# Last stage of two bottleneck blocks: the second block's last convolution with seven products for eight, on pairs of tiles

## The chip, the cores and the metric

The kernel runs on one core of one Trainium2 chip. The metric is device time in microseconds (us) of one execution. Of the kernel before, three runs are given: 2117.68, 2118.75 and 2119.07 us, so the median is 2118.75. One execution was recorded by the hardware profiler. Its span, from the first to the last instruction, is 2116.9 us, and the time of that execution is 2118.65 us.

## What is computed

Two equal blocks follow one another. The input is 64 images of 1024 channels and 14 x 14 pixels, in fp32. A block is, with the names of the reference:

```python
out = relu(bn(conv(x, w1, b1, 1, 0), g1, be1))     # 1x1, 1024 -> 256 channels
out = relu(bn(conv(out, w2, b2, 1, 1), g2, be2))   # 3x3, 256 -> 256
out = bn(conv(out, w3, b3, 1, 0), g3, be3)         # 1x1, 256 -> 1024
out = softplus(residual_scale)[0] * out
return relu(x + out)
```

`bn` normalises each channel with the mean and the variance of the whole batch. So nothing after a convolution can be finished before that convolution's statistics are complete, and the kernel falls into stages.

## The kernel before

**Tiles.** Channels lie on the 128 partitions. A tile is two images, 392 pixels (`PX`), and there are 32 tiles (`T`). A tile of x has 8 slots of 392 pixels (`CS`), one for each 128 of the 1024 channels; it is 1568 KB. A tile of the 256-channel data has two slots (`MS`) and stays in SBUF for all images, in `y_all`.

**Stages.** First comes the first convolution of block 0. Then, for each block: the 3x3 convolution; the Gram stage (`gram`, `conv3_stats`), which gets the mean and variance of the last convolution's result from products of its input, without computing it; and the last convolution with the residual. In block 0 the last convolution of a tile and the first convolution of block 1 run interleaved (`fused`). In block 1 nothing follows, so the last stage is plain: `residual` for one tile after the other. That is the stretch from about 1774 us to the end.

**The plain last stage.** For each tile, `residual` loads the tile of x from DRAM (`load_x`, on SP's DMA queue, in a ring of five buffers, `bufs=5` in `xpool`), makes for each of the 8 output slots two matmuls over the two input slots (`conv3`), adds the scaled result to x on VectorE (L837), applies the relu with the shift on ScalarE (L838), and stores the whole tile in one DMA from GpSimd's queue (L841). `Psum(scope, ["ps"], ps=5)` gives this stage five PSUM banks. The first two slots of tile 0 (`made`) are computed ahead of the statistics' end.

**Seven products for eight.** Taking two output slots, two input slots and two groups of columns, the last convolution is a 2 x 2 by 2 x 2 block product. Winograd's form of Strassen's scheme gets it with 7 block products in place of 8, at the price of sums of weights (`combine_w3`, made once), sums of columns (t1 to t4, for each group of columns) and partial results that are copied out and added later. The class `Seven` has the order of the products, `stream` interleaves one item with the item before it:

```python
            yield from now.p1()
            if before is not None:
                yield from before.p3()
                yield from before.p4()
            yield from now.p6()
            if before is not None:
                before.end()
            yield from now.p2()
            yield from now.p5()
            yield from now.p7()
```

One PSUM bank, `y`, takes p1, p6, p7 and p4 one on top of the other, and between them ScalarE copies its partial sums away (`saved`, L365 with the instruction at L265). The bank `p` takes p5 and p3; bank `x` takes p2. In `Conv3`, which `fused` uses, an item is one q of four (output slots q and q + 4) of one tile, and its columns are the two halves of the tile, 196 pixels each. After p2, p5, p3 and p4 VectorE adds a bank to x (`add`, L373). GpSimd adds the copies to x: after p3 for the first row (L399), after p7 for the second (L394). `end` does both relus on ScalarE.

**What sets the order.** Matmuls, and ScalarE's instructions issued by `act`, keep the order of the program (`keep_in_program_order`). The other engines' instructions are put in order by a scheduler when the kernel is built, and each engine then works through its list strictly in that order. DMAs of one queue are issued in order too: one that waits holds up those behind it. Five tiles of x can be in SBUF at once; a load into a buffer waits for the store of the tile that had it.

Of the kernel before, what the change touches and what calls it, by code (L numbers as in the profile page):

```python
# [34 lines left out]
FP = mybir.dt.float32  # L35
# [47 lines left out]
def bottlenecks(ctx: ExitStack, tc: tile.TileContext, x, w1s, w2s, w3s, pars, out):  # L83
# [19 lines left out]
    class Psum:  # L103


        def __init__(self, scope, cycle, **bufs):
            self.pool = scope.enter_context(tc.tile_pool(name="psum", bufs=1, space=bass.MemoryType.PSUM))
            self.cycle, self.bufs = itertools.cycle(cycle), bufs
# [5 lines left out]
    def load_x(pool, b, t, parts=1):  # L114
        xt = pool.tile([P, CS, PX], FP, tag="x", name=f"x_{b}_{t}")
        n = CS // parts
        for i in range(parts):
            nc.sync.dma_start(
                out=xt[:, i * n : (i + 1) * n, :].rearrange("p s f -> p (s f)"),
                in_=(x[t] if b == 0 else mids[t])[:, i * n * PX : (i + 1) * n * PX],  # L120
            )
        return xt
# [18 lines left out]
    def combine_w1(pool, w):  # L141
        return combine(pool, "w1", [[w[:, o, h] for h in range(2)] for o in range(MS)])

    def combine_w3(pool, w):
        n = CS // 2
        return combine(pool, "w3", [[w[:, s, o * n : (o + 1) * n] for s in range(MS)] for o in range(2)])
# [120 lines left out]
    class Conv1(Seven):  # L267
# [72 lines left out]
        def after7(self):  # L340
            self.result(1, 1, self.p, self.saved("au3"))

    class Conv3(Seven):

        prefix = "c"

        def __init__(self, psum, pool, xt, q, ys, sums, w3, aff, to):
            self.psum, self.pool, self.xt, self.n = psum, pool, xt, PX // 2  # L350
            self.o, self.to = (q, q + CS // 2), to
            (a, s), (self.scale, self.shift) = w3, aff
            self.a, self.s = [[w[:, q] for w in row] for row in a], [w[:, q] for w in s]
            self.b, (self.t1, self.t2, self.t3, self.t4) = ys, sums
            self.u12 = pool.tile([P, PX], FP, tag="cu12", name="cu12", bufs=2)

        def product(self, bank, w, b, start):
            matmul(
# [9 lines left out]
        def part(self, row, i):  # L368
            return self.xt[:, self.o[row], i * self.n : (i + 1) * self.n]
# [34 lines left out]
        def end(self):  # L404
            for row in range(2):
                self.relu(row)
            if self.to is not None:
                nc.scalar.dma_start(out=self.to, in_=self.xt.rearrange("p s f -> p (s f)"))

    def plain_conv1(psum, t, xt, a, par, stats):  # L410

# [413 lines left out]
        nc.vector.tensor_mul(sq, r[:, :, 1], r[:, :, 1])  # L825
        nc.vector.tensor_sub(mv[:, :, 1], r[:, :, 2], sq)

    def residual(psum, pool, b, t, w3, aff, made=()):

        scale, shift = aff  # L830
        xt = load_x(pool, b, t)
        to = mids[t] if b == 0 else out[t]
        step = 2 if b == 1 and t == T - 1 else CS
        for o in range(CS):
            ps = made[o] if o < len(made) else conv3(psum, t, o, w3)
            v = xt[:, o, :]
            nc.vector.scalar_tensor_tensor(v, ps, scale[:, o : o + 1], v, ALU.mult, ALU.add)  # L837
            nc.scalar.activation(v, v, AF.Relu, bias=shift[:, o : o + 1])  # L838
            if (o + 1) % step == 0:
                queue = nc.gpsimd if step == CS else nc.sync  # L840
                queue.dma_start(  # L841
                    out=to[:, (o + 1 - step) * PX : (o + 1) * PX],
                    in_=xt[:, o + 1 - step : o + 1, :].rearrange("p s f -> p (s f)"),
                )
        return xt

    def fused(psum, pool, xpool, first, w1, w3, aff, par, stats):


        xs = [first, load_x(xpool, 0, 1)]  # L850

        def last_convs():
            for t in range(1, T):
                if t + 1 < T:
                    xs.append(load_x(xpool, 0, t + 1))
                ys = [[two(t, s)[:, i * H // 2 : (i + 1) * H // 2] for i in range(2)] for s in range(MS)]
                sums = []
                for i in range(4):
                    v = pool.tile([P, PX // 2], FP, tag=f"ct{i}", name=f"ct{i}", bufs=2 if i > 1 else 1)
                    sums.append(v.rearrange("p (h l) -> p h l", l=G * W))  # L860
                t1, t2, t3, t4 = sums
                nc.vector.tensor_sub(t3, ys[1][1], ys[0][1])
                nc.vector.tensor_add(t2, t3, ys[0][0])
                nc.vector.tensor_sub(t1, ys[0][1], ys[0][0])
                nc.vector.tensor_sub(t4, ys[1][0], t2)
                for q in range(CS // 2):
                    yield Conv3(psum, pool, xs[t], q, ys, sums, w3, aff, mids[t] if q == CS // 2 - 1 else None)

        def first_convs():
            for t in range(T):  # L870
                yield Conv1(psum, pool, xs[t : t + 1], (t,), w1, par, stats)

        a, c = stream(first_convs()), stream(last_convs())
        for i in range(LAG):
            next(c)
        while True:
            more = next(a, "end"), next(c, "end")
            if more == ("end", "end"):
                break

    def stats_tile(n, name):
        return keep.tile([P, n, T, nc.vector.BN_STATS_DIM], FP, tag=f"stats{n}", name=name)
# [115 lines left out]
    for b in range(2):  # L998
        pb = par[b]
        sp = softplus(pb)  # L1000
        ccol = keep.tile([P, MS], FP, tag="ccol", name="ccol")
        nc.vector.tensor_scalar(ccol, pb[:, BE2 : BE2 + MS], 0.0, None, ALU.max)
        aff = affine(aggregate(stats1, T - 3 + b), MS, pb, G1, BE1)
        stats2 = keep.tile([P, MS, 1 + PARTS, nc.vector.BN_STATS_DIM], FP, tag="stats2", name=f"stats2_{b}")
        with tc.tile_pool(name=f"conv2_{b}", bufs=1) as pool, ExitStack() as scope:
            conv2(Psum(scope, ["ps"], ps=8), pool, b, pb, aff, stats2)

        with tc.tile_pool(name=f"last_{b}", bufs=1) as one, tc.tile_pool(
            name=f"last_x_{b}", bufs=4 if b == 0 else 5
        ) as xpool:  # L1010
            w3 = load_w3(one, b)
            if b == 0:
                w1 = load_w1(one, b + 1)
            aff = affine(aggregate(stats2, 0), MS, pb, G2, BE2)
            with ExitStack() as scope:
                if b == 0:
                    psum = Psum(scope, ["cy", "ay", "cx", "cy", "ay"], cy=2, ay=2)
                else:
                    psum = Psum(scope, ["ps"], ps=5)
                with tc.tile_pool(name=f"gram_{b}", bufs=1) as pool:  # L1020
                    crow = pool.tile([P, M], FP, tag="crow", name="crow")
                    nc.sync.dma_start(out=crow, in_=pars[b][:, NPAR:])
                    tc.keep_in_program_order(nc.vector.tensor_scalar(crow, crow, 0.0, None, ALU.max))

                    def piece(s, o):
                        spare = [xpool.tile([P, CS * PX], FP, tag="x", name="spare") for i in range(2)]
                        filters(1, s, o, spare)

                    weights = []
                    beside = {}  # L1030
                    if b == 0:
                        beside = {2 + 12 * i: partial(piece, i // MS, i % MS) for i in range(MS * MS)}
                        beside[NT - 5] = lambda: weights.extend((combine_w1(one, w1), combine_w3(one, w3)))
                    grams = gram(psum, pool, aff, crow, beside)
                    made = [conv3(psum, 0, o, w3) for o in range(2)]
                    mv3 = small.tile([P, CS, nc.vector.BN_AGGR_DIM], FP, tag="mv3", name="mv3")
                    conv3_stats(psum, pool, xpool, grams, w3, ccol, mv3)
                aff = affine(mv3, CS, pb, G3, BE3, conv_bias=B3)
                for a in aff:
                    nc.vector.tensor_scalar(a, a, sp, None, ALU.mult)  # L1040
                first = residual(psum, xpool, b, 0, w3, aff, made)
                if b == 1:
                    for t in range(1, T):
                        residual(psum, xpool, b, t, w3, aff)
                    return
                stats1 = stats_tile(MS, f"stats1_{b + 1}")
                with tc.tile_pool(name=f"conv1_{b + 1}", bufs=1) as pool:
                    fused(psum, pool, xpool, first, *weights, aff, par[b + 1], stats1)


# [39 lines left out]
```

## Time and profile before

| | |
|---|---|
| Median of three runs | 2118.75 us (2117.68 to 2119.07) |
| The profiled execution | 2118.65 us, its span 2116.9 us |
| TensorE, matmuls | 2068.3 us busy, 98% of the span |
| TensorE, weight loads (beside the matmuls) | 1747.9 us, 83% |
| VectorE | 1433.2 us, 68% |
| ScalarE | 814.2 us, 38% |
| GpSimd | 243.5 us, 12% |
| Mean DMA rate | 189 GB/s |
| L837, scaled add of a bank to x, 392 elements | 256 times, 626 ns |
| L838, relu, 392 elements | 264 times, 622 ns |
| Stores of the last stage (L841), 1568 KB each | 31, median 7.1 us to landing |
| Loads of x in the last stage, 1568 KB each | 32, median 7.6 us to landing |

How to read the profile: PE is TensorE's matmuls and PEld its weight loads, DVE is VectorE, ACT ScalarE, POOL GpSimd, SP the engine that only issues DMAs. A row of a group of instructions gives the line of the kernel, the engine, the operation, what it writes and reads with its shape, how often it ran, its busy time and the mean duration of one, and behind the last bar the time that the engine had been idle before such instructions, with what ended that wait. A row in order of time starts with the start in us and the duration in us; in brackets is the idle time ahead of it. An fp32 matmul is made of two passes and appears as two records.

### The profile page before, as it was taken

How to read it: one execution, taken by the hardware profiler on the slowest of the kernel's cores; microseconds unless marked ns; L12 is line 12 of the kernel's file. 1: busy time of each engine (PE TensorE's matmuls, PEld its weight loads, DVE VectorE, ACT ScalarE, POOL GpSimd, SP SyncE). 2: the span in 40 equal slices, each digit the busy share in tenths (PEclk: the TensorE clock that was granted, in tenths of full speed). 3: DMA queues.
4: the chain of work that ended last, by engine and by line, in shares of the span. 5: the costliest groups of instructions: out<-in, count | busy, mean ns of one | idle time of the engine just before them, and what ended most of it. 6: DMA issues, size and time to landing. Idle time of an engine off the chain costs nothing.

```text
span 2116.9 us, 27185 instructions
## 1 busy us (share of the span) xinstructions
PE 2068.3 (98%) x10368; PEld 1747.9 (83%) x10368; DVE 1433.2 (68%) x2778; ACT 814.2 (38%) x1579; POOL 243.5 (12%) x342
## 2 busy tenths in 40 slices
PE   8999989999989999999999999899999899999999
PEld 4555549999989889999999999799999897555555
DVE  5766559988866666666766667798888544444444
ACT  2211115233226055555555555523223402444444
POOL 0100000000001023333333333000000000000000
PEclk9999999999999999999999999999999999999999
DMA  7665425555543434444444443355554402778785
GB/s 292 250 211 209 163 90 192 201 191 184 200 159 118 155 150 159 177 183 161 175 160 176 183 160 145 120 214 184 190 208 180 194 1 99 306 277 325 282 321 215
DMA packets 45011, 400.00 MB, mean 189 GB/s; under 512 B 5584, under 2 KB 5840, under 8 KB 12240
## 3 DMA queue, kind: packets, MB, share of 16 engines
q1 hardware_dynamic: 30528, 280.28, 37.0%
q0 software_dynamic: 8448, 66.07, 7.7%
q10 hardware_dynamic: 5904, 51.91, 5.9%
q8 instruction: 82, 1.34, 0.3%
q14 instruction: 49, 0.40, 0.1%
HBM read 280.79 MB, written 117.44 MB: 188 GB/s over the span
## 4 chain that ended last, share of the span: by engine, by line
PE 93%; DVE 3%; ACT 2%; DMA 1%; issue 1%; POOL 0%; SPq 0%; DVEq 0%; ACTq 0%
PE ps L155 17%; PE ps L573 17%; PE ay L155 14%; PE ps L550 8%; PE cy L155 8%; PE ap L155 8%; PE ax L155 4%; PE cp L155 4%; PE ps L560 3%; PE cp L755 3%; PE cx L155 2%; PE ap L756 2%; ACT y L427 1%; PE ps L773 1%; DMA y<-in_w 0%
## 5 line engine op out<-in xcount | busy, mean ns | idle before, releaser
L573 PE MATMUL ps<-r,u 128*128 128x224 f32 (+1 forms) x2048 | 391.2, 343 | 14.1 <-DVE r L506 14.1
L573 PEld LDWEIGHTS ps<-r,u 128*128 128x128 f32 x2048 | 372.1, 190 | 18.9 <-DVE r L506 7.9
L155 PE MATMUL ps<-y,w 128*128 128x392 f32 x1024 | 340.5, 496 | 0.0
L155 PEld LDWEIGHTS ps<-y,w 128*128 128x128 f32 x1024 | 195.9, 191 | 143.5 <-issue 2.8
L837 DVE SCALAR_TENSOR_TENSOR x<-ps,scale,x 128x392 f32<-128x392 f32 x256 | 160.0, 626 | 175.5 <-PE ps L155 171.8
L265 ACT ACTIVATE cu<-cy,scale 128x196 f32<-128x196 f32 x372 | 154.0, 423 | 221.2 <-PE cy L155 221.2
L838 ACT ACTIVATE x<-x,shift 128x392 f32<-128x392 f32 x264 | 163.6, 622 | 183.7 <-DVE x L837 183.7
L155 PE MATMUL ay<-at,w1s 128*128 128x196 f32 (+1 forms) x752 | 209.7, 382 | 1.2 <-ACT au L265 1.0
L605 ACT ACTIVATE ms<-ps 128x448 f32<-128x448 f32 (+1 forms) x80 | 40.5, 506 | 333.7 <-PE ps L550 323.3
L155 PEld LDWEIGHTS ay<-at,w1s 128*128 128x128 f32 x752 | 136.0, 190 | 36.6 <-ACT au L265 4.6
L550 PE MATMUL ps<-sums,u 128*128 128x224 f32 (+1 forms) x768 | 158.6, 337 | 0.0
L265 ACT ACTIVATE x<-x,shift 128x392 f32<-128x392 f32 x248 | 140.9, 614 | 28.3 <-POOL x L399 28.3
L399 POOL TENSOR_TENSOR x<-x,cu 128x392 f32<-128x392 f32 x124 | 125.9, 1015 | 188.1 <-DVE x L373 188.0
L373 DVE SCALAR_TENSOR_TENSOR x<-cp,scale,x 128x196 f32<-128x196 f32 x248 | 103.4, 417 | 63.7 <-PE cp L155 63.7
L550 PEld LDWEIGHTS ps<-sums,u 128*128 128x128 f32 x768 | 131.5, 189 | 0.1
L155 PE MATMUL cy<-ct,w3s 128*128 128x196 f32 x496 | 123.0, 330 | 1.4 <-ACT cu L265 1.4
L755 PE MATMUL cp<-zt 128*128 128x257 f32 x392 | 120.6, 389 | 2.9 <-DVE zt L775 2.4
L265 ACT ACTIVATE au<-ay 128x196 f32<-128x196 f32 (+1 forms) x141 | 53.8, 381 | 167.2 <-PE ay L155 164.6
L155 PE MATMUL ap<-x,w1s 128*128 128x196 f32 (+1 forms) x376 | 107.7, 390 | 5.4 <-DVE y L311 5.4
L427 ACT ACTIVATE y<-y,shift,scale 128x1568 f32<-128x1568 f32 (+2 forms) x68 | 103.6, 1584 | 5.6 <-DVE shift L934 5.6
L155 PE MATMUL ax<-x,w 128*128 128x196 f32 (+1 forms) x376 | 104.8, 381 | 0.0
L155 PE MATMUL ay<-x,w 128*128 128x196 f32 (+1 forms) x376 | 104.8, 381 | 0.0
(226 smaller groups left out, 3429.2 us busy)
## 6 DMA issues: line engine op xcount, KB each, us to landing
x<-in_x SPq DMA_DIRECT2D x62, 1568.0 KB, 6.6
u<-u SPq DMA_DIRECT2D x64, 1280.0 KB, 5.5
x<-mid SPq DMA_DIRECT2D x32, 1568.0 KB, 7.6
mid<-x ACTq DMA_DIRECT2D x31, 1568.0 KB, 5.1
out<-x POOLq DMA_DIRECT2D x31, 1568.0 KB, 7.1
u<-u SPq DMA_DIRECT2D x32, 1024.0 KB, 4.8
u<-y POOLq DMA_DIRECT2D x16, 320.0 KB, 6.2
u<-spare POOLq DMA_DIRECT2D x16, 320.0 KB, 2.7
```

What stands on the lines that cost most here:

```text
L155: tc.keep_in_program_order(nc.tensor.matmul(*args, **kw))
L265: tc.keep_in_program_order(nc.scalar.activation(*args, **kw))
L373: nc.vector.scalar_tensor_tensor(v, bank, self.scale[:, o : o + 1], v, ALU.mult, ALU.add)
L399: nc.gpsimd.tensor_add(v, v, self.u12)
L427: nc.scalar.activation(y, y, AF.Relu, bias=shift[:, s : s + 1], scale=scale[:, s : s + 1])
L550: nc.tensor.matmul(to[:, o, :n], u[:, s, o, k], v[:, s].rearrange("p l c -> p (l c)"), start=(s == 0), stop=(s == MS - 1),)
L560: nc.tensor.matmul(to, u[:, s, o, k], v, start=(s == 0), stop=(s == MS - 1))
L573: nc.tensor.matmul(to, u[:, s, o, k], v, start=start, stop=stop, skip_group_check=by_slot)
L755: nc.tensor.matmul(g0, zt[:, c, 0:P], zt[:, c, :], start=first, stop=last)
L756: nc.tensor.matmul(g1, zt[:, c, P:M], zt[:, c, P:], start=first, stop=last)
L837: nc.vector.scalar_tensor_tensor(v, ps, scale[:, o : o + 1], v, ALU.mult, ALU.add)
L838: nc.scalar.activation(v, v, AF.Relu, bias=shift[:, o : o + 1])
```

## The change

The last stage is rewritten for tiles 1 to 30. Tiles 0 and 31 stay plain.

- `final` takes the tiles in 15 pairs. A pair's columns are its two tiles, 392 pixels each, so `Conv3Pair` is `Conv3` with n = 392 in place of 196. There are four items for a pair, one for each q, and an item has seven products.
- The column sums t1 to t4 become a function, `column_sums`, that both stages use. In the last stage they are 392 elements wide, and made once for a pair.
- `Conv3Pair.after3` has GpSimd add the two copies to x in two instructions of 392, since the two tiles are not one piece of memory. `after7` is inherited: another add of 392 on GpSimd.
- `Conv3Pair.end` does the relu of the first row on ScalarE, two instructions of 392, and that of the second row on VectorE, two `tensor_scalar` (add the shift, maximum with 0).
- The stores go out per item: for each of the two tiles one DMA of the two slots q and q + 4 (392 KB, rows of 1568 bytes), on SP's queue. Before it was one DMA of 1568 KB per tile on GpSimd's queue.
- Five loads of x are issued ahead; after the first item of each pair, loads up to four tiles ahead of the pair's first are issued.
- PSUM in this stage has banks cy (2), cx (2), cp (2), and single ones for the Gram stage; the plain tiles draw on cy and cx, four banks, where they had five.
- `combine_w3` is now also made for block 1, beside the Gram stage, at its fifth step from the end.

```diff
+    def column_sums(pool, ys, n):
+        sums = []
+        for i in range(4):
+            v = pool.tile([P, n], FP, tag=f"ct{i}", name=f"ct{i}", bufs=2 if i > 1 else 1)
+            sums.append(v.rearrange("p (h l) -> p h l", l=G * W))
+        t1, t2, t3, t4 = sums
+        nc.vector.tensor_sub(t3, ys[1][1], ys[0][1])
+        nc.vector.tensor_add(t2, t3, ys[0][0])
+        nc.vector.tensor_sub(t1, ys[0][1], ys[0][0])
+        nc.vector.tensor_sub(t4, ys[1][0], t2)
+        return sums
...
+    class Conv3Pair(Conv3):
+        def part(self, row, i):
+            return self.xt[i][:, self.o[row], :]
+
+        def after3(self):
+            self.add(0, 1, self.p)
+            for i in range(2):
+                v = self.part(0, i)
+                nc.gpsimd.tensor_add(v, v, self.u12[:, i * self.n : (i + 1) * self.n])
+
+        def end(self):
+            for i in range(2):
+                o, v = self.o[0], self.part(0, i)
+                act(v, v, AF.Relu, bias=self.shift[:, o : o + 1])
+            for i in range(2):
+                o, v = self.o[1], self.part(1, i)
+                nc.vector.tensor_scalar(v, v, self.shift[:, o : o + 1], 0.0, ALU.add, ALU.max)
+            q, step = self.o[0], CS // 2
+            for i in range(2):
+                nc.sync.dma_start(
+                    out=self.to[i].rearrange("p (s f) -> p s f", s=CS)[:, q::step, :], in_=self.xt[i][:, q::step, :]
+                )
...
+    def final(psum, pool, xpool, xs, a, w3, aff):
+        def pairs():
+            for t in range(1, T - 1, 2):
+                ys = [[two(t + i, s) for i in range(2)] for s in range(MS)]
+                sums = column_sums(pool, ys, PX)
+                for q in range(CS // 2):
+                    yield Conv3Pair(psum, pool, xs[t : t + 2], q, PX, ys, sums, w3, aff, out[t : t + 2])
+                    if q == 0:
+                        for i in range(len(xs), min(t + 5, T)):
+                            xs.append(load_x(xpool, 1, i))
+
+        for _ in stream(pairs()):
+            pass
+        residual(psum, xs[T - 1], 1, T - 1, a, aff)
...
-                    psum = Psum(scope, ["ps"], ps=5)
+                    psum = Psum(scope, ["cy", "cx"], cy=2, cx=2, cp=2)
...
+                    beside = {NT - 5: combined}
...
-                first = residual(psum, xpool, b, 0, w3, aff, made)
-                if b == 1:
-                    for t in range(1, T):
-                        residual(psum, xpool, b, t, w3, aff)
-                    return
+                xs = [load_x(xpool, b, t) for t in range(2 if b == 0 else 5)]
+                residual(psum, xs[0], b, 0, w3, aff, made)
+                with tc.tile_pool(name=f"rest_{b}", bufs=1) as pool:
+                    if b == 1:
+                        final(psum, pool, xpool, xs, w3, *weights, aff)
+                        return
```

## The prediction

> **What bounds the kernel now.** I read the page's busy shares first, then the table by stretches for the last stage (everything from about 1774 us on), then the order of time inside one tile of it, then the rows of single operations, and at last the places of the fused stage in the middle where GpSimd and VectorE work at once. Columns of the table: stretch, length, then busy us of TensorE, its weight loads, VectorE, ScalarE, GpSimd; granted clock, DMA share, GB/s.
>
> ```profile
> 1850.00:1900.00 50.00, 50.00 (x154) 28.85 (x153) 23.80 (x39) 23.62 (x38) 2.65 (x5) 1.00 0.78 294
> 1900.00:1950.00 50.00, 50.00 (x154) 28.85 (x152) 23.75 (x39) 23.62 (x38) 2.66 (x5) 1.00 0.85 316
> 1950.00:2000.00 50.00, 50.00 (x153) 28.88 (x152) 23.75 (x39) 23.62 (x38) 2.66 (x5) 1.00 0.77 280
> ```
>
> TensorE never rests, the others are half idle, and DMA is busy 0.77 to 0.85. Inside a tile:
>
> ```profile
> 1881.67 0.53 POOL L841 DMA_DIRECT2D out<-x  x1 [10.00 <-ACT x L838]
> 1882.72 0.63 DVE L837 SCALAR_TENSOR_TENSOR x<-ps,scale,x 128x392 f32<-128x392 f32 x1 [0.64 <-PE ps L155]
> 1884.04 0.63 DVE L837 SCALAR_TENSOR_TENSOR x<-ps,scale,x 128x392 f32<-128x392 f32 x1 [0.69 <-PE ps L155]
> 1892.20 0.53 POOL L841 DMA_DIRECT2D out<-x  x1 [10.00 <-ACT x L838]
> ```
>
> One store to the next is 10.53 us for a tile of 16 products: 0.658 us each. So the stage is bound by TensorE: a pair of tiles takes 21.06 us, and the 30 tiles that change take 315.9 us. The operations that the change uses:
>
> ```profile
> L265 ACT ACTIVATE x<-x,shift 128x392 f32<-128x392 f32 x248 | 140.9, 614 | 28.3 <-POOL x L399 28.3
> L399 POOL TENSOR_TENSOR x<-x,cu 128x392 f32<-128x392 f32 x124 | 125.9, 1015 | 188.1 <-DVE x L373 188.0
> L431 DVE TENSOR_SCALAR y<-y,scale,shift 128x896 f32<-128x896 f32 x2 | 1.5, 747 | 0.1
> L432 DVE TENSOR_SCALAR y<-y 128x896 f32<-128x896 f32 x2 | 1.3, 626 | 0.1
> ```
>
> And three places of the fused stage, in order of time:
>
> ```profile
> 753.12 0.96 DVE L338 TENSOR_TENSOR at<-x,at 128x784 f32<-128x784 f32 x1
> 753.43 1.11 POOL L394 TENSOR_TENSOR x<-x,cu 128x196 f32<-128x196 f32 x1 [2.07 <-ACT cu L265]
> 754.51 1.00 POOL L399 TENSOR_TENSOR x<-x,cu 128x392 f32<-128x392 f32 x1
> ...
> 1102.99 1.02 POOL L399 TENSOR_TENSOR x<-x,cu 128x392 f32<-128x392 f32 x1 [0.45 <-DVE x L373]
> 1103.82 0.41 DVE L863 TENSOR_TENSOR ct<-ct,y 128x196 f32<-128x196 f32 x1 [0.24 <-PE cy L155]
> 1104.26 0.36 DVE L865 TENSOR_TENSOR ct<-y,ct 128x196 f32<-128x196 f32 x1
> ```
>
> L394 takes 0.60 in the mean of its row, but 1.11 where a VectorE sum with both inputs in SBUF had begun 0.31 us before it: it stood until that sum was through. The reverse is L863: 0.41 where GpSimd was still at work, 0.35 to 0.36 for its like (L865) alone, in all 30 of its later rounds. So GpSimd lets VectorE in about 0.83 + 0.05 = 0.88 us after its own start. The scaled adds with one input in PSUM (L373) last 0.42 beside GpSimd or not.
>
> **What the Trainium skill says.** "SBUF — State Buffer", section "Who interferes with whom": GpSimd's only SBUF ports are VectorE's second pair; a VectorE instruction with two SBUF inputs, or one in a 2-port mode, and a GpSimd instruction exclude each other, the later one waits for the whole of the earlier. The rows above agree for two inputs (1.11 for 0.60). "VectorE: DVE Perf Modes", section "Mode 2×_2P": fp32 operations with one tensor and a scalar, SBUF to SBUF, run two results a cycle through that pair. L432 agrees: 626 ns for 896 elements is less than one a cycle. That such an operation also shuts GpSimd out, no place of this trace shows. "DMA: Bandwidth & Descriptors", section "Specifications": rows from 512 B up go at line rate. The packets of the trace agree roughly: median 469 ns for 12544 B, 124 for 3136, 84 for 2048, 46 for 1024.
>
> **The change part by part.** An item is a pair of tiles and one q of four: seven products p1 to p7.
>
> TensorE: 28 products for 32 per pair, 28 x 0.658 = 18.42 us for 21.06, which is 15 x 2.64 = 39.5 us less if it never waits.
>
> ScalarE per item: three copies out of PSUM (about 0.62, the duration of the same size in L838) and two relus, 5 x 0.62 = 3.1 of 4.61 us. It fits.
>
> VectorE per item: four scaled adds of 0.63 (0.535 when one follows the other: three of L837 took 1.69), two relus, and per pair four sums. A relu with one scalar from SBUF: L432 fits 896/1.92 + 160 ns, L431 has two such scalars and 120 more, so 204 + 160 + 60 = 0.42, 0.33 in a row. Sums of 392 lie between 0.50 (336) and 0.62 (448): 0.56, 0.475 in a row. Busy 4 x 0.535 + 0.66 + 0.475 = 3.3 of 4.61.
>
> GpSimd per item: three adds of 392 (V0, G11, V1), 3.05 us, 0.98 apart at best (754.51 less 753.43 + 1.11 is -0.03). Per pair that is 12.2 us, where the stage had nothing but issues.
>
> No engine is full, but they are chained, and orders are fixed. As built, VectorE has per item: A00 (add after p2), A11 (after p5), R11 (relu), A01 (after p3), A10 (after p4), R10 (relu); GpSimd has V0 (needs A00), G11 (needs A11 and ScalarE's copy after p7), V1 (needs A01). R11 needs G11. R10 comes up while V1 holds the ports. Next item's A00 stands behind R10. The round, with handovers of 0.09 VectorE to GpSimd (1102.91 to 1102.99) and 0.05 back: A00 0.63 + 0.09, V0 0.98, G11 1.02 + 0.05, R11 0.33, A01 0.63 + 0.09, V1's hold 0.88, R10 0.33: 5.03 us, over TensorE's 4.61. In a pair the sums come in twice: one between A10 and R10 of the third q, again after V1's hold (+0.48); three between A11 and A01 of the last, which take turns with V0 and G11 (counted from A00's end: the first waits for V0 until 0.97, G11 for it until 1.44, the second for G11 until 2.3, so A01 starts at 3.25 in place of 2.14 + 0.33 = 2.47: +0.75). Pair: 4 x 5.03 + 1.23 = 21.35 us, of 18.42 that TensorE needs. 15 x (21.35 - 21.06) = +4.4 us. What then is late is p3 of each item, which waits for A11, so TensorE idles some 0.7 us per item.
>
> Around it: the first two pairs' five sums are scheduled into the short chain of eight-element operations after the statistics (1774.24 to 1776.87), 5 x 0.5 = +2.5 us on the first add; with four banks for the plain tile where five stood, TensorE is through its two free banks at 1774.06 + 2.63 = 1776.7 and waits for the first add's end, 1777.5 + 2.5 = 1780.0: +3.4 us, none before. combine_w3 is four sums of 0.69 (2.5 in a row) in the Gram stage, where VectorE has 1.06 us idle of 1.75 and the copy's user another 0.86: +0.7.
>
> Stores and loads: 8 stores per pair on SP's queue between the loads, 128 packets of 1568 B per engine in place of 16 of 12544. Their time lies between 59 ns (in proportion to 12544) and 70 (to 1024); I take 66 between 46 and 84. Per pair and engine: loads 16 x 0.469 = 7.5, stores 128 x 0.066 = 8.4 (7.5 to 9.0), 15.9 of 21.35 us: hidden. A load waits on SP for the last stores of the tile whose buffer it takes, behind at most one store of the next pair; it is issued about an item into a pair and its tile is needed one to two pairs' starts later, some 14 us for the 7 that a landing takes. The last tile is as before: 0.
>
> Sum: +4.4 + 3.4 + 0.7 = +8.5, less about 1 us because the first items run at TensorE's pace before the round takes hold: +7.5. On the profiled span 2116.9 that is 2124.4; its own time was 1.75 above its span (2118.65), and the median of the runs 0.1 above that: 2126 us.
>
> **The rivals.** (1) The ports don't bind, or hardly. Then A01, A10, R10 follow at once (0.535 + 0.535 + 0.33 = 1.40, where A01, V1's hold and R10 made 1.93), the round is 4.5, TensorE's 4.61 rules with some 0.1 lost at its edges: 18.8 a pair, 15 x 2.26 - 4.1 = 30 us faster, 2089. Against it stands the 1.11 of L394. (2) The ports bind for relus alone, or are given back sooner than the 0.88: 19.6 to 20.1 a pair, 14 us faster, 2105. For it: the only long wait is a single one, and spans on GpSimd are rough. It decides below 20.8 us a pair, a round of about 4.9, only 0.13 from mine. (3) DMA becomes the bound: packets over (21.35 - 7.5) / 128 = 108 ns, or loads held up behind stores in one queue. At 130 ns a pair is 24.1: +46 + 4, 2168; a milder wait gives 2140 to 2150. For it: the share of 0.85 now, and one queue for both directions. Against: 124 ns is what twice the bytes took. (4) GpSimd's adds lengthen to 1.1 (beside the relus): the round 5.2, 2133. I count it with the main case.
>
> **How the numbers follow.** The forecast case 0.60 (own range 2115 to 2137), rival 1 0.07, rival 2 0.19, rival 3 0.14. I count 0.2% (4.2 us) as what a measurement can tell from none. Of the main case 0.06 falls below 2114.5, 0.16 within, 0.38 above 2123. So faster 0.06 + 0.07 + 0.19 = 0.32, same 0.16, slower 0.38 + 0.14 = 0.52. The range 2100 to 2144 leaves out rival 1, and tails of rivals 2 and 3.
>
> **What would show it.** Right: in the last stage TensorE busy about 0.86, pairs 21.3 us apart; p3 waiting for VectorE's L386; VectorE relus (L441) or sums that last far beyond 0.42 and 0.56 or begin late after GpSimd; GpSimd near 0.6 busy. Wrong: TensorE full with 18.5 us a pair (rival 1), L441 never above 0.45 beside GpSimd (rival 2), VectorE's adds waiting for x from DMA (rival 3).

## The result, and the profile after

The changed kernel takes 2124.0 us (median of four runs, 2122.6 to 2125.6) where the kernel before takes 2118.9 (2117.7 to 2121.2): 1.0023 times as long, 95% interval 1.0005 to 1.0040. That is slower, by little, and 2 us from the 2126 forecast. The profiled execution took 2125.6 us with a span of 2123.8.

The table by stretches for the last stage of the changed kernel, with the columns of the table shown for the kernel before:

```profile
1850.00:1900.00 50.00, 45.88 (x130) 23.33 (x128) 40.00 (x69) 26.43 (x48) 28.46 (x28) 1.00 0.82 293
1900.00:1950.00 50.00, 46.58 (x133) 24.36 (x134) 36.76 (x65) 25.99 (x47) 29.68 (x29) 1.00 0.81 287
1950.00:2000.00 50.00, 46.84 (x135) 24.27 (x133) 38.38 (x67) 27.42 (x49) 28.89 (x28) 1.00 0.87 313
```

TensorE, full before, has 130 to 135 matmul records in 50 us where it had 154; VectorE went from 23.8 to about 38 us, GpSimd from 2.7 to 29. No engine is full any more, and DMA's share (0.77 to 0.85 before) is much the same. What each engine waits for in the stage (window 1800 to 2100; engine, what waits, for whom: us in all, times, longest):

```profile
POOL x L433 <- DVE x L386: 119.6, 109, 1.5
ACT cu L265 <- PE cy L155: 108.6, 58, 2.2
DVE x L441 <- POOL x L407: 70.2, 43, 1.9
PEld cp L155 <- DVE x L386: 56.8, 56, 1.4
```

The waits make a ring: VectorE's relu R11 (L441) waits for GpSimd's G11 (L407), GpSimd's V0 and V1 (L433) for VectorE's adds (L386), and TensorE's p3 (its bank cp) for A11. One round of it in order of time, TensorE's and ScalarE's rows left out but for p3:

```profile
1941.67 0.61 DVE L386 SCALAR_TENSOR_TENSOR x<-cx,scale,x 128x392 f32<-128x392 f32 x1
1942.21 0.61 DVE L386 SCALAR_TENSOR_TENSOR x<-cp,scale,x 128x392 f32<-128x392 f32 x1
1942.42 1.01 POOL L433 TENSOR_TENSOR x<-x,cu 128x392 f32<-128x392 f32 x1 [0.89 <-DVE x L386]
1942.88 0.93 PE L155 MATMUL cp<-y,w3s 128*128 128x392 f32 x2 [0.70 <-DVE x L386]
1943.39 1.01 POOL L407 TENSOR_TENSOR x<-x,cu 128x392 f32<-128x392 f32 x1
1944.43 0.42 DVE L441 TENSOR_SCALAR x<-x,shift 128x392 f32<-128x392 f32 x1 [1.61 <-POOL x L407]
1944.78 0.62 DVE L386 SCALAR_TENSOR_TENSOR x<-cp,scale,x 128x392 f32<-128x392 f32 x1
1945.31 0.61 DVE L386 SCALAR_TENSOR_TENSOR x<-cy,scale,x 128x392 f32<-128x392 f32 x1
1945.47 1.02 POOL L433 TENSOR_TENSOR x<-x,cu 128x392 f32<-128x392 f32 x1 [1.07 <-DVE x L386]
1945.96 0.75 DVE L441 TENSOR_SCALAR x<-x,shift 128x392 f32<-128x392 f32 x1
1946.63 0.61 DVE L386 SCALAR_TENSOR_TENSOR x<-cx,scale,x 128x392 f32<-128x392 f32 x1
```

From A00 (cx) at 1941.67 to the next A00 at 1946.63 is 4.96 us, over the 4.61 that TensorE needs for seven products. The two relus are the thing to see: R11, with GpSimd at rest, takes 0.42; R10, come up while V1 is under way, takes 0.75. The groups of operations by shape say the same for the whole window (count | busy, mean ns | idle before):

```profile
L441 DVE TENSOR_SCALAR x<-x,shift 128x392 f32<-128x392 f32 x113 | 58.2, 515 | 71.6 <-POOL x L407 70.2
L353 DVE TENSOR_TENSOR ct<-y,ct 128x392 f32<-128x392 f32 x14 | 19.2, 1373 | 0.0
L352 DVE TENSOR_TENSOR ct<-y 128x392 f32<-128x392 f32 x14 | 15.7, 1124 | 0.0
L351 DVE TENSOR_TENSOR ct<-ct,y 128x392 f32<-128x392 f32 x14 | 15.0, 1068 | 0.0
L350 DVE TENSOR_TENSOR ct<-y 128x392 f32<-128x392 f32 x13 | 7.2, 553 | 0.0
```

A column sum that finds GpSimd at rest takes 0.55 (L350); the other three take up to 1.37, since they stand until a GpSimd add is through.

Below, "items" are the mean distances from one p3 to the next, for the first to the fourth q of a pair, read from the starts of p3 in the trace. In the changed kernel they are 4.96, 4.98, 5.48 and 5.83: a pair of 21.25 us, where two tiles took 21.06.

### The profile page after: what moved, and what is told of

Read it like the earlier page. It is cut to its first block, busy times and chain, and to the rows that moved or that the text cites. A ratio compares the mean times of both kernels' runs of the same rounds, so it can differ in the third digit from the quotient of the medians.

```text
span 2123.8 us, 27779 instructions
## 1 busy us (share of the span) xinstructions
PE 2051.5 (97%) x10248; PEld 1720.7 (81%) x10248; DVE 1528.9 (72%) x2962; ACT 834.4 (39%) x1639; POOL 413.7 (19%) x492
## 4 chain that ended last, share of the span: by engine, by line
PE 78%; DVE 10%; DMA 4%; POOL 3%; ACT 2%; issue 2%; POOLq 0%; DVEq 0%; SPq 0%; ACTq 0%
PE ps L611 17%; PE ay L155 14%; PE cy L155 9%; PE ps L588 8%; PE ap L155 8%; PE ax L155 4%; PE cp L155 4%; DVE x L386 4%; PE ps L598 3%; PE cp L793 3%; PE cx L155 3%; DMA out<-x 3%; POOL x L407 2%; DVE x L441 2%; PE ap L794 2%
## 5 line engine op out<-in xcount | busy, mean ns | idle before, releaser
L265 ACT ACTIVATE cu<-cy,scale 128x196 f32<-128x196 f32 (+1 forms) x552 | 257.9, 476 | 341.1 <-PE cy L155 335.4
L265 ACT ACTIVATE x<-x,shift 128x392 f32<-128x392 f32 x368 | 214.9, 615 | 59.5 <-POOL x L433 31.1
L386 DVE SCALAR_TENSOR_TENSOR x<-cp,scale,x 128x196 f32<-128x196 f32 (+1 forms) x368 | 177.1, 481 | 66.1 <-PE cp L155 66.1
L155 PE MATMUL cy<-ct,w3s 128*128 128x196 f32 (+1 forms) x736 | 221.7, 383 | 2.5 <-ACT cu L265 2.5
L407 POOL TENSOR_TENSOR x<-x,cu 128x196 f32<-128x196 f32 (+1 forms) x184 | 140.2, 762 | 199.7 <-ACT cu L265 117.9
L155 PEld LDWEIGHTS cy<-ct,w3s 128*128 128x128 f32 x736 | 133.6, 190 | 36.9 <-ACT cu L265 3.8
L412 POOL TENSOR_TENSOR x<-x,cu 128x392 f32<-128x392 f32 x124 | 125.8, 1015 | 188.1 <-DVE x L386 188.0
L433 POOL TENSOR_TENSOR x<-x,cu 128x392 f32<-128x392 f32 x120 | 123.5, 1029 | 129.2 <-DVE x L386 123.4
L155 PE MATMUL cp<-y,w3s 128*128 128x196 f32 (+1 forms) x368 | 120.0, 408 | 22.8 <-DVE x L386 20.2
L155 PE MATMUL cy<-y,w 128*128 128x196 f32 (+1 forms) x416 | 132.0, 405 | 0.1
L386 DVE SCALAR_TENSOR_TENSOR x<-cx,scale,x 128x196 f32<-128x196 f32 (+1 forms) x184 | 88.7, 482 | 54.6 <-PE cx L155 54.5
L155 PE MATMUL cx<-y,w 128*128 128x196 f32 (+1 forms) x404 | 125.5, 396 | 0.0
```

The lines of the kernel that those rows point to most:

```text
L155: tc.keep_in_program_order(nc.tensor.matmul(*args, **kw))
L265: tc.keep_in_program_order(nc.scalar.activation(*args, **kw))
L386: nc.vector.scalar_tensor_tensor(v, bank, self.scale[:, o : o + 1], v, ALU.mult, ALU.add)
L407: nc.gpsimd.tensor_add(self.part(1, 1), self.part(1, 1), u3)
L412: nc.gpsimd.tensor_add(v, v, self.u12)
L433: nc.gpsimd.tensor_add(v, v, self.u12[:, i * self.n : (i + 1) * self.n])
```

## The experiments

### Which part of the round holds it

Two theories first. Mine: VectorE and GpSimd exclude each other at SBUF, and this, with VectorE's fixed order, makes the round. The rival: VectorE simply has too much to do in a row. Four edits of the changed kernel tell them apart.

All relus on ScalarE:

```
-                nc.vector.tensor_scalar(v, v, self.shift[:, o : o + 1], 0.0, ALU.add, ALU.max)
+                act(v, v, AF.Relu, bias=self.shift[:, o : o + 1])
```

> All four relus of an item on ScalarE, the rest as in the changed kernel. Theory (the round A00, V0, G11, R11, A01, V1's hold, R10 sets the item): without R11 and R10 VectorE's list no longer waits for GpSimd, ScalarE has 7 x 0.535 to 7 x 0.62 = 3.7 to 4.3 of 4.61 us, so TensorE sets the item: about 4.7 us, 18.8 for a pair in place of 21.25, 15 x 2.45 = 37 us less than the changed kernel: about 2088, ratio to before 0.985 to 0.989. Rival a (GpSimd's three adds or the DMA set the item, the relus don't matter): item stays at 5.3 in the mean, 2121 to 2127. Rival b (ScalarE becomes the bound, u3 late): 5.0 or more.

Measured: 2103.0 us, 0.9925 of before (0.9910 to 0.9940). Items 5.37, 4.79, 4.85, 4.71: 19.72 a pair. The ring is open and the kernel is faster than both, but 15 us of the expected gain are missing. In order of time on ScalarE, and TensorE's p4:

```profile
1934.26 0.59 ACT L265 ACTIVATE cu<-cy,scale 128x392 f32<-128x392 f32 x1 [1.20 <-PE cy L155]
1934.74 2.15 ACT L265 ACTIVATE x<-x,shift 128x392 f32<-128x392 f32 x4
1936.79 1.04 ACT L265 ACTIVATE cu<-cy,scale 128x392 f32<-128x392 f32 x2
1937.42 0.30 PEld L155 LDWEIGHTS cy<-ct,w 128*128 128x128 f32 x2 [0.53 <-ACT cu L265]
```

Four relus stand in one row, 2.15 us, ahead of the third copy u3; p4 needs the bank that u3 empties, and waits. A limit moved to an engine that is busy 36 of 50 us: order, not load. These rows are from an item of 4.79. The longest item, the first of a pair with 5.37, holds more than half of what is lost (0.76 of 1.28 us a pair over four items of 4.61), and there the column sums have a part. The last two sums before it take turns with GpSimd (L350, 1.37), V1 comes late, the relus wait for V1, and p4 waits for the copy behind them:

```profile
1927.42 1.37 DVE L350 TENSOR_TENSOR ct<-y 128x392 f32<-128x392 f32 x1
1930.47 1.65 ACT L265 ACTIVATE x<-x,shift 128x392 f32<-128x392 f32 x3 [0.59 <-POOL x L433]
1932.64 0.93 PE L155 MATMUL cy<-ct,w 128*128 128x392 f32 x2 [0.60 <-ACT cu L265]
```

The relu on VectorE, but as an operation that takes its zero from a bank of zeros in PSUM:

```
-                nc.vector.tensor_scalar(v, v, self.shift[:, o : o + 1], 0.0, ALU.add, ALU.max)
+                nc.vector.scalar_tensor_tensor(v, v, self.shift[:, o : o + 1], self.zeros, ALU.add, ALU.max)
```

> VectorE's relu takes the maximum with a bank of zeros in PSUM (one input in SBUF, no 2-port mode), so each is longer, 0.61 for 0.42. Theory (the port pair): its duration is 0.61 beside GpSimd too, and an item without column sums takes 0.72 + 0.98 + 1.07 + 4 x 0.535 = 4.9 us, a little less than now (4.97) although 0.4 us of VectorE's work is added. Rival (R10 waits for data, not for ports): relus still last up to 0.75 and more where V1 runs, and an item takes 4.97 + 0.4 = 5.4, in all 60 x 0.4 = 24 us slower than the changed kernel. In the third and fourth item of a pair the column sums still wait for GpSimd, some 5.8 us each by the theory, so the whole stays within 8 us of the changed kernel.

Measured: 2119.1 us, 1.0000 of before (0.9992 to 1.0009). Items 4.71, 4.61, 5.15, 6.48. The group of this relu, and then, in order of time, two of them beside V1 (L433):

```profile
L441 DVE SCALAR_TENSOR_TENSOR x<-x,shift,ap 128x392 f32<-128x392 f32 x116 | 66.7, 615 | 1.1
```

```profile
1946.36 1.02 POOL L433 TENSOR_TENSOR x<-x,cu 128x392 f32<-128x392 f32 x1 [0.17 <-DVE x L386]
1946.98 1.16 DVE L441 SCALAR_TENSOR_TENSOR x<-x,shift,ap 128x392 f32<-128x392 f32 x2
```

This relu is longer than the one it replaces, 0.615 for 0.42, and yet the two items without sums fall from 4.96 and 4.98 to 4.71 and 4.61. So VectorE's load is not what makes the round: the rival falls. The sections "Who interferes with whom" of "SBUF — State Buffer" and "Why PSUM operands drop a tier" of "VectorE: DVE Perf Modes" in the Trainium skill say that a VectorE instruction with one SBUF input outside the 2-port modes doesn't contend with GpSimd, and that any PSUM operand keeps fp32 at one result a cycle; all 120 of them lie between 0.61 and 0.62 us, beside V1 or not, which agrees with the first; for the second it only fits that they are longer than 0.42, since the edit also changes the operation. The scheduler changed the order too: R11 and R10 now stand one behind the other after A10, so that A01 no longer waits for G11 through R11. So the edit isn't the lock alone, and how much of the shorter items is the order was not tried. The sums still take turns (L353 1.37 as in the changed kernel), and cost more in it.

The column sums made for the first pair alone; the 56 sums of the other fourteen pairs are left out, and their products use the first pair's:

```
-                sums = column_sums(pool, ys, PX)
+                sums = column_sums(pool, ys, PX) if t == 1 else sums
```

> The column sums are made for the first pair only and used for all (the sums of the other 14 pairs are left out). Theory: third and fourth item fall from 5.48 and 5.83 to the 4.97 of the others; 14 x 1.37 = 19 us less than the changed kernel, 2105, ratio to before 0.993. Rival (the sums hide in VectorE's waits): 2122 to 2126.

Measured: 2105.1 us, 0.9934 of before (0.9918 to 0.9951); items 4.96, 4.98, 4.98, 4.97. The round without sums is 4.97 in all four items, and the sums are worth 18.9 us by the times (19.7 by the items, 15 x 0.51 + 14 x 0.86), though they are only 4 x 0.56 = 2.2 us of work for a pair of 21.

One store for a whole tile, after a pair's last item, in place of one per slot:

```
-            q, step = self.o[0], CS // 2
-            for i in range(2):
-                nc.sync.dma_start(
-                    out=self.to[i].rearrange("p (s f) -> p s f", s=CS)[:, q::step, :], in_=self.xt[i][:, q::step, :]
-                )
+            for i in range(2 if self.o[0] == CS // 2 - 1 else 0):
+                nc.sync.dma_start(out=self.to[i], in_=self.xt[i].rearrange("p s f -> p (s f)"))
```

> One store for each whole tile after a pair's last item, on SP's queue, in place of eight for a pair. Theory (DMA is hidden in the changed kernel): the items keep their lengths in the first half of a pair; rows of 12544 B save at most some us of DMA time, but the two stores land about 8 us later and the load behind them with them, some 26 us after the pair's start, just when it is needed: 0 to +3 us for a pair, 2122 to 2165. Rival (the small rows of the changed kernel hold it up): faster, by up to 15 x 1 us, 2108.

Measured: 2124.7 us, 1.0028 of before (1.0018 to 1.0038); items 4.96, 4.97, 5.48, 5.83, those of the changed kernel. Stores are hidden in either form. DMA's share between 1850 and 2000 us falls from between 0.81 and 0.87 to between 0.71 and 0.79.

### Where the rest of the first run's gain went, and the start

Relus on ScalarE, two behind the next item's first copy and two behind its second (`mid` is called by the stream right after p1):

```
+        def relus(self, *parts):
+            for row, i in parts:
+                o, v = self.o[row], self.part(row, i)
+                act(v, v, AF.Relu, bias=self.shift[:, o : o + 1])
+
+        def mid(self):
+            self.relus((0, 0), (1, 1))
+
         def end(self):
-            for i in range(2):
...
+            self.relus((0, 1), (1, 0))
```

> All four relus of an item on ScalarE, as in the run with relus on ScalarE, but not in one row after the second copy: two of them (slot q of the first tile, slot q+4 of the second) follow the next item's first copy, the other two its second copy. Theory: what that run still lost beside its 2088 is ScalarE's order alone. Four relus of 0.54 to 0.61 stood in front of the third copy (u3), 2.15 us in a row, u3 came 0.6 us late, and p4 waited for it. With two and two, each pair of relus has the 2 us between two copies: ScalarE is busy 7 x 0.6 = 4.2 of 4.61 us an item and the copies are on time. Items of 4.61 to 4.75, a pair 18.6 to 19.0 us in place of 19.73, 15 x 0.7 to 1.1 less than 2103: 2086 to 2092 (ratio 0.985 to 0.987). Rival S: VectorE's sums, which take turns with GpSimd, hold the third and fourth item as before; a pair 19.2 to 19.7, 2095 to 2102. Rival D: DMA is the bound now (its share was 0.84 to 0.93 at 19.73 us a pair, some 17.5 us of work a pair): waits for x from DMA on VectorE or GpSimd grow beyond 10 us in all and a pair stays at 19.3 or more, 2097 to 2103.

Measured: 2098.6 us, 0.9899 of before (0.9884 to 0.9914); items 4.61, 4.68, 5.42, 4.71. As built here, the relu of the first part runs before GpSimd's add of the first copy, so the kernel does not compute the whole of what it should (nor do the next one and the run with both edits). Three items come near TensorE's pace, the third does not. GpSimd's order is now G11 (L412), V0, V1 (both L438), since V0 had to come behind the relu; the three run in one row, and the sums of the third item (L356, L358) fall into it. In order of time there:

```profile
1938.39 1.02 POOL L412 TENSOR_TENSOR x<-x,cu 128x392 f32<-128x392 f32 x1 [1.72 <-ACT cu L270]
1939.33 0.62 DVE L391 SCALAR_TENSOR_TENSOR x<-cy,scale,x 128x392 f32<-128x392 f32 x1
1939.38 2.31 POOL L438 TENSOR_TENSOR x<-x,cu 128x392 f32<-128x392 f32 x2
1939.99 0.83 DVE L356 TENSOR_TENSOR ct<-ct,y 128x392 f32<-128x392 f32 x1
1940.86 1.26 DVE L358 TENSOR_TENSOR ct<-y,ct 128x392 f32<-128x392 f32 x1
1942.04 0.61 DVE L391 SCALAR_TENSOR_TENSOR x<-cx,scale,x 128x392 f32<-128x392 f32 x1
```

L356 waits for V0, V1 for L356, L358 for V1, and A00 (cx) starts 2.71 us after A10 (cy).

The same with sums for the first pair alone (56 sums left out again, and the relu ahead of the add again):

> Relus on ScalarE in two pairs, and the column sums made for the first pair alone (the other fourteen pairs' 56 sums are left out, so their products use the first pair's sums). Theory: with the relus gone from VectorE the sums find room; the difference to the run with the relus split is under 3 us. Rival S: it is 8 to 14 us faster than that run, at 2084 to 2088, items all alike at 4.61 to 4.65. Rival D (DMA): no difference, both stay at 2097 or more.

Measured: 2089.3 us, 0.9855 of before (0.9840 to 0.9869); items 4.69, 4.69, 4.66, 4.69; TensorE busy 50.00 of 50 us. The difference of 9.3 us is what the column sums cost in this order, and by the items nearly all of it lies in the third (5.42 and 4.66).

The start. In the changed kernel alone, the first pair's sums put behind the fourth to seventh add of tile 0:

```
-            nc.vector.scalar_tensor_tensor(v, ps, scale[:, o : o + 1], v, ALU.mult, ALU.add)
+            add = nc.vector.scalar_tensor_tensor(v, ps, scale[:, o : o + 1], v, ALU.mult, ALU.add)
+            if steps:
+                tc.keep_in_program_order(add)
+                if 2 < o < 7:
+                    tc.keep_in_program_order(steps[o - 3]())
```

> The changed kernel with one thing moved: the four column sums of the first pair are no longer free to run in the chain of small operations after the statistics, but stand one by one behind the fourth to seventh add of tile 0 (VectorE has 0.69 us free of 1.32 there); the first sum of the second pair follows there too. Theory (my step on the start): the five sums cost the first add 1.6 to 2.5 us and TensorE 2.7 us of waiting; they go, since the sums now lie in VectorE's free time: 2121.3 (2120.5 to 2122), 1.001 of before. Rival: TensorE's wait at the start comes from four banks in place of five, and not from the sums; then 2123 to 2124, 1.002.

Measured: 2124.0 us, 1.0021 of before (1.0013 to 1.0029): nothing gained. The first add does come 1.6 us earlier, counted from the end of the last 128x1 product (2.66 us after it, 4.26 in the changed kernel). But TensorE never waited for it. Tile 0's products in the changed kernel, and below in this one:

```profile
1778.05 2.96 PE L155 MATMUL cx<-y,w 128*128 128x392 f32 x4
1780.80 2.75 PE L155 MATMUL cy<-y,w 128*128 128x392 f32 x4
1783.39 1.48 PE L155 MATMUL cx<-y,w 128*128 128x392 f32 x4
```

```profile
1776.91 2.96 PE L155 MATMUL cx<-y,w 128*128 128x392 f32 x4
1779.66 2.75 PE L155 MATMUL cy<-y,w 128*128 128x392 f32 x4
1782.25 1.48 PE L155 MATMUL cx<-y,w 128*128 128x392 f32 x4
```

The third row begins 5.34 us after the first in both. The first two rows take twice the time of the third, because the granted clock was one half; the table by stretches of the changed kernel (the column before DMA's share):

```profile
1775.00:1777.00 2.00, 2.00 (x19) 2.00 (x18) 0.00 (x0) 0.00 (x0) 0.00 (x0) 0.88 0.00 0
1777.00:1779.00 2.00, 2.00 (x8) 1.68 (x9) 0.78 (x5) 0.00 (x0) 0.00 (x0) 0.50 0.00 0
1779.00:1781.00 2.00, 2.00 (x5) 1.05 (x4) 2.00 (x11) 0.30 (x1) 0.00 (x0) 0.50 0.97 270
1781.00:1783.00 2.00, 2.00 (x5) 0.81 (x3) 1.86 (x10) 0.00 (x0) 0.00 (x0) 0.50 0.96 389
1783.00:1785.00 2.00, 2.00 (x6) 1.16 (x6) 1.76 (x5) 1.90 (x4) 0.00 (x0) 0.91 0.34 144
```

and a stretch of the kernel before, where tile 0's products begin at 1774.06:

```profile
1777.00:1779.00 2.00, 2.00 (x5) 1.05 (x4) 1.55 (x3) 1.48 (x3) 0.00 (x0) 0.50 1.00 414
```

Both edits together:

> Both: relus on ScalarE in two pairs, and the first pair's column sums behind tile 0's adds. If the two are independent, it is 2 to 3 us below the run with the relus split alone: 2083.5 to 2090 where that is 2086 to 2092. If the start is taken up by a later wait (DMA as the bound), no difference.

Measured: 2098.7 us, 0.9900 of before (0.9885 to 0.9915), where the split alone took 2098.6. The miss is the same one: there was nothing to gain at the start.

### A version that reaches TensorE's pace

The split with V0 ahead of its relu (the computation is whole again):

```
+        def copied(self, i):
+            v = self.part(0, i)
+            nc.gpsimd.tensor_add(v, v, self.u12[:, i * self.n : (i + 1) * self.n])
+
+        def after2(self):
+            self.add(0, 0, self.x)
+            self.copied(0)
+
         def after3(self):
             self.add(0, 1, self.p)
...
+            self.copied(1)
```

> The relus on ScalarE in two pairs again, now with GpSimd's first add of an item (V0) standing ahead of the first of these relus, as the computation asks (in the two runs before with the split, the relu of the first part ran ahead of the add of the first copy, so V0 waited for it: 92.7 us of waits of L412 for ScalarE in the stage). If V0's wait mattered, this is up to 4 us faster than 2098.6; if, as the items of 4.61 to 4.69 say, only the column sums of the third item still hold the stage, it is the same within 2 us: pairs of 19.3 to 19.5 us, the third item 5.3 to 5.45.

Measured: 2090.7 us, 0.9865 of before (0.9849 to 0.9882); items 4.92, 4.61, 4.69, 4.71, a pair of 18.93. That is 7.9 us better, twice what I allowed, and the third item is no longer the slow one. I had also misread L412 for V0: it is G11, and its waits for ScalarE are those for u3. What V0's place did is in the rows that answer to those above:

```profile
1936.43 0.63 DVE L391 SCALAR_TENSOR_TENSOR x<-cy,scale,x 128x392 f32<-128x392 f32 x1
1936.47 1.01 POOL L436 TENSOR_TENSOR x<-x,cu 128x392 f32<-128x392 f32 x1 [0.34 <-DVE x L391]
1937.08 0.83 DVE L356 TENSOR_TENSOR ct<-ct,y 128x392 f32<-128x392 f32 x1
1937.94 0.57 DVE L358 TENSOR_TENSOR ct<-y,ct 128x392 f32<-128x392 f32 x1
1938.43 0.62 DVE L391 SCALAR_TENSOR_TENSOR x<-cx,scale,x 128x392 f32<-128x392 f32 x1
```

V0 has gone ahead of G11, V1 stands here alone, L358 finds GpSimd at rest, and A00 starts 2.00 us after A10. So most of the 9.3 us that the sums cost in the other order was not their price but that of GpSimd's three adds in one row; what is left, 0.31 us, is in the item behind the last two sums.

The next pair's sums one to an item, behind A10:

```
+        def after4(self):
+            self.add(1, 0, self.y)
+            if self.todo:
+                tc.keep_in_program_order(self.todo.pop(0)())
```

> The last kernel, and the four column sums of the next pair one to an item, each right behind VectorE's last add of that item (A10), where GpSimd has its rest, in place of four within the third and fourth item; all four in two buffers. Theory: a sum takes its turn with GpSimd as before, but 3 GpSimd adds and one sum are 3.05 + 0.56 = 3.6 us of port time in an item of 4.61, where the third item had 3.05 + 4 x 0.56 = 5.3. Then no item waits for sums: 4.61 to 4.7, a pair 18.5 to 18.8, like the run with sums made once (18.73): 2086 to 2090, ratio 0.984 to 0.986, faster than both kernels. Rival: each sum waits for V1 and puts off the next item's first add by 0.2 to 0.5 us; then all items are 4.8 to 5.0, a pair 19.2 to 20.0, 2096 to 2108.

Measured: 2083.4 us, 0.9831 of before (0.9816 to 0.9846); items 4.61, 4.61, 4.58, 4.61: 18.40 a pair, what 28 products of 0.658 take. It beats both kernels, the changed one by 40 us. Two more things differ: t1 and t2 have a second buffer like t3 and t4, and VectorE's four adds are kept in the order of the program; their order in the trace, A00, A11, A01, A10, is the same as in the run before. Its stretches, and two of its four sums (the others have the same mean):

```profile
1900.00:1950.00 50.00, 50.00 (x153) 28.88 (x152) 35.50 (x55) 41.50 (x77) 32.94 (x33) 1.00 0.96 336
1950.00:2000.00 50.00, 50.00 (x153) 28.88 (x152) 35.22 (x55) 41.69 (x77) 32.85 (x34) 1.00 1.01 362
```

```profile
L439 DVE TENSOR_TENSOR ct<-y 128x392 f32<-128x392 f32 x14 | 13.3, 948 | 0.0
L440 DVE TENSOR_TENSOR ct<-y,ct 128x392 f32<-128x392 f32 x14 | 13.3, 947 | 0.0
```

Every sum still stands behind V1 (0.95 for 0.56); now nobody waits for it. VectorE is as busy as in the run before (35 us of 50), and TensorE is full again.

The same with whole stores:

> The last one, and one store for a whole tile after a pair's last item in place of a store per slot. DMA's share was 0.93 to 0.98 where TensorE was full. If packets of 1568 B hold the stage at that pace, this is 2 to 5 us faster than the kernel with spread sums (pair 18.45 in place of 18.7). If stores are hidden still, it is the same within 1.5 us, or up to 4 us slower, since the last pair's stores start late and loads wait longer for the buffers.

Measured: 2083.1 us, 0.9831 of before (0.9816 to 0.9846), the items the same. DMA's share falls from between 0.95 and 1.01 to between 0.86 and 0.91, and the time does not move: stores by slot fill DMA at this pace, but nothing waits for them yet for long (4.0 us in 260 in all engines' waits for DMA, none with whole stores).

## Why the prediction was right, and where it was not

**The round** was predicted at 5.03 us and is 4.96. Term by term from the rows above, start to start, the prediction's figure in brackets: A00 to V0 0.75 (0.72), V0 to G11 0.97 (0.98), G11 to R11 1.04 (1.07), R11 to A01 0.35 (0.33), A01 to V1 0.69 (0.72), V1 to the next A00 1.16 (1.21). That the relu and a GpSimd add keep each other out, which no place of the trace before showed, is seen in the 0.75 beside V1 for the 0.42 alone, and in the run with zeros in PSUM, whose relus go in beside V1 and last as long as elsewhere; that this is a 2-port mode fits, but no trace names it. Without those 0.33 the round would be 4.63 (an estimate from these rows), hardly over TensorE's 4.61.

**The column sums** in the third and fourth item were +0.48 and +0.75 (by the prediction's own figures 3.25 - 2.47 = 0.78) and are +0.51 and +0.86. The pair: 21.35 forecast, 21.25 measured. The last pair makes no sums for another, so one of the 15 is shorter, which the prediction overlooked: from the first p3 to the last, 59 items, it is 312.84 us, where as much of the plain stage, 59 quarters of 21.06, is 310.64. That is +2.2 us for +4.4. A tenth of a microsecond in a pair is 1.5 us in the kernel, and the sign of this term hung on 0.2. The forecast had the mechanism; that its sum came out on the right side of zero is also luck of that size.

**The start** failed: "TensorE is through its two free banks at 1774.06 + 2.63 = 1776.7 and waits for the first add's end" took the clock of the middle of the stage. Over tile 0's first products the granted clock is 0.50 in the kernel before too (0.50 from 1775 to 1779), so two banks last 5.3 us, and the first add, which ends 4.88 us after the last 128x1 product in the changed kernel, is just in time. The step's first half was nearly right (the first add 1.6 us later, 2.5 forecast, since some sums run where the small operations wait for each other); its second, +3.4, is 0. In place of it, from the last 128x1 product to the last ScalarE instruction the kernel takes 338.90 us before and 342.15 after: +3.25, of which the pairs are 2.2. The remaining 1.05 lies at the edges, and there the first item's p6 waits 1.2 us for u1, which stands behind tile 0's last relu on ScalarE; the forecast had no such wait. The ramp for which it took off 1 us is 0.26: the first item has 4.70 where later ones have 4.96.

**The Gram stage** was +0.7; from its first to its last L775 (L813 after) it is +0.4 (85.37 to 85.77 us), and the statistics behind it, to the end of the last 128x1 product, +0.6 (15.95 to 16.55), which I had not forecast. Of that, 0.4 lies in the 128x1 products (from the start of the first to the end of the last 2.25 and 2.65 us), during which the clock falls to 0.50: 0.8 us before their end in the kernel before, 1.7 us in the changed one. For the rest, that stage's pools of PSUM banks changed too; whether it is that was not tried.

**The sum**, then: +7.5 forecast; +1.0 + 2.2 + 1.05 = +4.3 found in the stages from the Gram stage on, of a difference of the medians of 5.1. The profiled spans differ by more, 6.9, because the profiled execution after reached the Gram stage 3.0 us later than that before (1675.87 against 1672.88). Of these, 1.9 are there by the first 200 matmul records, 75 us into the program, far from anything that the change touches. The whole-store kernel, which shares everything but the stores with the changed one, reached the stage at 1672.79 us; in the other ten kernels it lies between 1673.7 and 1675.1. Single executions vary by that much (the spans of the changed kernel's four are 2120.8 to 2123.8), and these can't say whether the change delays that part at all; the last 0.8 us are not placed. The errors of the start and of the pair go the same way, the missed wait of p6, the missed statistics and the ramp the other: that 2126 lies only 2 us from the result is in part luck.

**DMA** was hidden, as said. Its work was sized too small: 15.9 us a pair forecast, 0.83 x 21.25 = 17.7 by the share, 0.75 x 21.25 = 16.0 with whole stores. The 66 ns for a packet of 1568 B is right: between 1800 and 2060 us the median is 66 and the mean 70, far under the 108 from which it decides. The loads were too small: their packets of 12544 B have the median of 469 that the prediction took, but a mean of 560. With the means, 16 x 0.56 + 128 x 0.07 = 17.9.

**The rivals.** That the ports don't bind (TensorE full, 2089) and that they bind little (below 20.8 us a pair) are out by the 21.25 and the 0.75; DMA as the bound is out by whole stores, which change nothing. The size of rival 1 was sound: with the ring open and the orders put right the kernel does run at TensorE's 18.4, at 2083. In the experiments, I was wrong twice in the same way: when the ring opened, the next limit was a place in a fixed list (u3 behind four relus, V0 behind G11), not the load of an engine.

## What to carry to other kernels

When work is moved to GpSimd, list for each VectorE instruction beside it whether it has two SBUF inputs or runs in a 2-port mode, and lay them one behind the other with GpSimd's, in VectorE's fixed order: the length of that round, and not the busy share of any engine, is what to hold against TensorE's time. A cure need not be fewer operations: a longer relu with one operand in PSUM (which also changed the order), or the same sums put where nobody waits for them, gave back what the short ones cost. Before a stall is priced at the head of a stage, look up the granted clock of that very stretch.

## What the runs showed that I had not expected

TensorE's granted clock fell to 0.50 while its records show it busy 2.00 of 2.00 us: while and after 32 matmul records of 128x2 and 16 of 128x1 ran. The Trainium skill, "TensorE: Matmul & The Clock Gate", section "What's actually happening", ties the half rate to how busy TensorE has been of late; what these runs add is that the clock was not kept up over such narrow products, though they fill the record, in the kernel before as in the one after, and also behind the same products of block 0 (0.50 from 740 to 742 us before). The half rate lasted 6.8 us in the last stage of both kernels (1773.4 to 1780.2 before, 1776.5 to 1783.3 after), of which the wide products behind ran 5 to 6 us at half speed. No run changes the narrow products, so that they are the cause is not shown.

By the records a GpSimd add keeps VectorE out for less than it lasts, where the section that the prediction cites speaks of the whole instruction (its own sums took 0.88); the measurement decides here, but spans on GpSimd are rough. A sum that came up during V1 got in 0.88 us after V1's start (1.02 long) in the kernel with spread sums, and R10 0.82 after it in the changed kernel, reckoned back from the end with the durations that each has alone.
